# Order of the last share, home of the second residual weights, and engines of the last image in a four-layer kernel

## The chip, the cores and the metric

The kernel runs on one core of one Trainium2 chip. The metric is the device time of one execution in microseconds (us); the text compares medians of several runs, and reads the details from one profiled execution.

## The reference, cut to what matters

Two images of 128 channels and 64 x 64 pixels go through four layers:

```python
x = L0(x)   # group norm, 4-head attention over 4096 pixels, projection, residual
x = L1(x)   # deformable convolutions, below
x = L2(x)   # three residual steps, below
x = L3(x)   # layer norm, selective scan in four directions, projection, residual

# end of layer 1
out = silu(affine(conv2d(concatenate([o0, ox, oy], axis=1), fuse_w, 0), fuse_g, fuse_b))
n = out.shape[2] * out.shape[3] - 1
d = (out - out.mean(axis=(2, 3), keepdims=True)) ** 2
e = d / (4.0 * (d.sum(axis=(2, 3), keepdims=True) / n + 0.0001)) + 0.5
out = out * sigmoid(e)
return out + x

# layer 2
for _ in range(3):
    t = relu(conv(x, w1) + b1)
    x = x + (1.0 / 3.0) * (conv(t, w2) + b2)
return relu(x)
```

The 1 x 1 convolution of layer 1 over three concatenated inputs is a sum of three shares. The two 3 x 3 convolutions of layer 2 have their own weights w1 and w2, used in each of three steps.

## The kernel before

**Engines and order.** PE multiplies matrices, DVE, ACT and POOL do elementwise work, SP issues nearly all DMAs. Each engine works through its own queue in order. Most stages stand under `tc.manual_schedule()`: the order of the Python calls is the order on each engine. A tile that is made where an older pool's tiles lay waits until that pool's instructions are done.

**The attention** (`attend`, layer 0) walks through units (batch b, head h, block of queries qb, block of keys kb), three blocks of keys at a time: `scores` on PE, exponential on ACT, `weigh` on PE, and at the end of each qb `normalise` on DVE and POOL. The queries and keys of the next head are fetched in pieces at qb 1 to 4 of the head before it. At qb 5 to 7 of batch 0, head 3, the kernel loads the three rows of taps of w1 (`residual_taps`, on SP, into the two-buffer pool of the pieces) and combines them on DVE (`residual_weights`, which calls `quad_weights` with ten instructions) into `g.u1`. The 3 x 3 convolutions of layer 2 are computed four columns at a time from six combinations of columns and six combinations of weights, hence the 6 in `u1`.

**The last share** (end of `snakes`, layer 1). For each of eight jobs, one batch and two row blocks j and j + 1, `last_share` gives four parts: `silu` (ACT line 1094, then PE line 1100 into PSUM), `add` (DVE line 1105, two instructions, into the image `xa`), `fused` (ACT line 1109, Silu in place on the image), and `stats` (DVE line 1113, two instructions; after a batch's last job `gate_stats`, lines 1165 to 1169). `by_column` shows the image as four planes of every fourth column, so that the row blocks of one batch lie between one another in memory, and the two batches lie apart. The jobs are put one step apart:

```python
jobs = [last_share(b, j, c) for b in range(NB) for j in range(0, NBLK, 2)]
for n in range(len(jobs) + 3):
    for k in range(4):
        if 0 <= n - k < len(jobs):
            jobs[n - k][k]()
```

**Layer 2** (`layer2`) first makes the gate of layer 1: squares and sigmoids on ACT (lines 1286, 1287), product and sum on DVE (1291, 1292), with the layer's input `gt` loaded on SP (line 1285). Then `products` (PE line 1311) multiplies six combined images `v[j][b]` with six combined weights, `outputs` (lines 1320 to 1347) turns the six results into four columns on ACT and DVE, and `combine` (DVE, lines 1259 to 1270) with `differences` (POOL) prepares the next convolution. `later` runs a combine one turn late. Convolution j is 0 with weights `g.u1` and 1 with weights `u2`; the taps of w2 are loaded as `raw` into a free part of `v[1][1]`, and `quad_weights` (lines 1178 to 1187) makes `u2` from them between `products(0, 1, 1)` and the combines behind it. In the last step both halves k of an image stand in `mid[0]` and `mid[1]`, and after k = 1 two Relus on ACT (line 1347) write them back into the image `xa` in its usual order of pixels, which means with a stride of four elements. Relus of the two batches are made alike.

**Layer 3** (`layer3`) begins with loads of weights on SP, small set-up on DVE (`onesm`, line 1452) and a layer norm that starts on PE (line 1519); then it runs 64 blocks whose loads are `dd`, `b` and `c`.

Of the kernel before, what the change touches and what calls it, by code (L numbers as in the profile page):

```python
# [10 lines left out]
F32 = mybir.dt.float32  # L11
# [9 lines left out]
P = 128  # L21
# [51 lines left out]
def vec(g, name):  # L73
    i = VI[name]
    return g.vecs[:, i : i + 1]
# [6 lines left out]
def layer0(g, I):  # L82
# [6 lines left out]
    with ExitStack() as ctx:  # L89
# [213 lines left out]
        with cond.Else():  # L303
            nc.gpsimd.memset(v3[1][:, :, :, 3 * CH :], 1.0)
            with tc.tile_pool(name="l0vs", bufs=2) as vs, tc.tile_pool(name="l0vp", bufs=2, space=PSUM) as vp:
                for k in range(NBLK):
                    late_values(g, v3, vp.tile([P, BLK], F32, name="pv"), vs, wv, 1, k)
                for y in range(3):
                    residual_weights(g, y, residual_taps(g, I, vs, y))
            nc.vector.memset(g.last[0:96], 0.0)  # L310
            nc.vector.memset(g.last[96:128], 1.0)
            nc.vector.memset(g.heads, 0.0)
            attend_any(g, I, v3, qd, kd, q4)
# [14 lines left out]
    return t  # L328


def residual_taps(g, I, pool, y):

    t = pool.tile([P, PIECE], F32, name="piece")[:, : 3 * P].rearrange("p (x o) -> p x o", o=P)
    g.nc.sync.dma_start(t, I["w1T"][:, 3 * y : 3 * y + 3, :])
    return t


def residual_weights(g, y, t):

    quad_weights(g, g.u1[:, y : y + 1], t.unsqueeze(1), 1.0)  # L340


def normalise(g, acc, rec, parts, dst):
# [60 lines left out]
def attend(g, I, v3, wv, qd, kd, q4, qk, stg):  # L404


    nc, tc = g.nc, g.tc
    NS = L // P
    GR = 3
    LAG = 2  # L410
    with ExitStack() as ctx:
        ap = ctx.enter_context(tc.tile_pool(name="l0ap", bufs=1))
        sm = ctx.enter_context(tc.tile_pool(name="l0asm", bufs=2))
        ep = ctx.enter_context(tc.tile_pool(name="l0ep", bufs=5))
        pss = ctx.enter_context(tc.tile_pool(name="l0pss", bufs=2, space=PSUM))
        psa = ctx.enter_context(tc.tile_pool(name="l0psa", bufs=2, space=PSUM))

        att = {}

        def scores(group):  # L420
            ps = pss.tile([P, GR, BLK], F32, name="ps")
            for i, (b, h, qb, kb) in enumerate(group):
                t = qk[h % 2]
                nc.tensor.matmul(  # L424
                    ps[:, i, :], t[:, 1, kb * P : (kb + 1) * P], t[:, 0, qb * BLK : (qb + 1) * BLK],
                    start=True, stop=True,
                )
            e = ep.tile([P, GR, BLK], F16, name="e16")
            n = len(group)
            nc.scalar.activation(e[:, :n, :], ps[:, :n, :], AF.Exp, scale=1.0 / UP**2)  # L430
            return e

        acc = None

        def weigh(group, e):
            nonlocal acc
            for i, (b, h, qb, kb) in enumerate(group):
                if kb == 0:
                    acc = psa.tile([P, BLK], F32, name="acc")
                nc.tensor.matmul(acc, v3[b][:, kb, h, :], e[:, i, :], start=(kb == 0), stop=(kb == NS - 1))  # L440
                if kb == NS - 1:
                    finish(b, h, qb, acc)

        def finish(b, h, qb, acc):

            if qb == h == 0:
                att[b] = ap.tile([P, L], F32, name="att")
            final = (b, qb) == (NB - 1, NBLK - 1)
            if final and h == NH - 1:
                nc.scalar.copy(g.last, acc)  # L450
                return
            to = g.heads if final else att[b][:, qb * BLK : (qb + 1) * BLK]
            rec = sm.tile([P, BLK], F32, name="rec")
            parts = sm.tile([CH, 3, BLK], F32, name="parts")
            normalise(g, acc, rec, [parts[:, j, :] for j in range(3)], to[h * CH : (h + 1) * CH])
            if h == NH - 1:
                done.append((b, qb))

        def pieces(n, qb):

            if n == 0 and qb == 0:
                return [(0, 0, 1), (0, 0, 2)]
            if n == 0 and qb == 5:
                return [(0, 0, 3)]
            if n + 1 < NB * NH and 1 <= qb <= 4:
                return [(n + 1, 1, qb - 1), (n + 1, 0, qb - 1)]
            return []

        units = [
            (b, h, qb, kb) for b in range(NB) for h in range(NH) for qb in range(NBLK) for kb in range(NS)  # L470
        ]
        held, done, coming = [], [], []
        taps = None
        with tc.manual_schedule():
            nc.gpsimd.memset(v3[1][:, :, :, 3 * CH :], 1.0)
            for c in range(1, 4):
                split_less(g, qk[0], 1, c, q4[1][:, c * PIECE : (c + 1) * PIECE], nc.vector)
            for u in range(0, len(units), GR):
                group = units[u : u + GR]
                b, h, qb, kb = group[0]  # L480
                held.append((group, scores(group)))
                if done and 24 <= kb < 24 + GR:
                    b0, q0 = done.pop(0)
                    project(g, b0, q0, psa.tile([P, BLK], F32, name="acc"), att[b0][:, q0 * BLK : (q0 + 1) * BLK])
                if len(held) > LAG:
                    weigh(*held.pop(0))
                if b == 0 and 1 <= h <= 2 and qb in (0, 5, 6, 7) and 24 <= kb < 24 + GR:
                    k = 4 * (h - 1) + (0, 5, 6, 7).index(qb)
                    late_values(g, v3, psa.tile([P, BLK], F32, name="acc"), sm, wv, 1, k)
                if 4 <= kb < 4 + GR:  # L490
                    coming = [(n, j, c, fetch(g, stg, (qd, kd)[j], n, c)) for n, j, c in pieces(b * NH + h, qb)]
                    if (b, h) == (0, NH - 1) and qb >= 5:
                        taps = qb - 5, residual_taps(g, I, stg, qb - 5)
                elif 26 <= kb < 26 + GR:
                    for n, j, c, t in coming:
                        split(g, qk[n % 2], j, c, t)
                    coming = []
                    if taps:
                        residual_weights(g, *taps)
                        taps = None  # L500
            for x in held:
                weigh(*x)
            assert not done
# [435 lines left out]
def snakes(g, ctx, hz, ahead, fw):  # L939
# [179 lines left out]
    with tc.manual_schedule():  # L1119
# [30 lines left out]
        c, steps = affine(1, st)  # L1150
        for f in steps:
            f()
        jobs = [last_share(b, j, c) for b in range(NB) for j in range(0, NBLK, 2)]
        for n in range(len(jobs) + 3):
            for k in range(4):
                if 0 <= n - k < len(jobs):
# [33 lines left out]
def layer2(g, I):  # L1190
# [14 lines left out]
    with ExitStack() as ctx:  # L1205
# [8 lines left out]

        mid = [a.tile([P, 4, RP, NS], F32, name=f"mid{i}") for i in range(2)]

        raw = v[1][1].rearrange("p x r i -> p (x r i)")[:, 4 * HW * NS : 4 * HW * NS + 9 * P]
        nc.sync.dma_start(raw, I["w2T"].rearrange("p t o -> p (t o)"))
        u2 = a.tile([P, 3, NX, P], F32, name="u2")
        weights = (g.u1, u2)  # L1220
        first = [
# [8 lines left out]
        def inner(t):  # L1230
            return t[:, :, :, 0:NQ]
# [73 lines left out]
        def products(j, b, k):  # L1305
# [8 lines left out]
                    )  # L1314
            return m

        def outputs(step, j, b, k, m):
            s, p = (wk.tile([P, BLK], F32, name=f"m{i}", bufs=2) for i in range(2))
            d, q = (wk.tile([P, BLK], F32, name=f"t{i}") for i in (3, 4))
            nc.scalar.activation(s, m[1], AF.Identity, bias=vec(g, "b1") if j == 0 else b23)  # L1320
            nc.scalar.copy(p, m[3])
            nc.vector.tensor_sub(d, s, m[2])
            nc.vector.tensor_add(s, s, m[2])
            nc.vector.tensor_sub(q, p, m[4])
            nc.vector.tensor_add(p, p, m[4])
            t = mid[k % 2]
            y = [t[:, c, :, 0:NQ] for c in range(4)]
            stt = nc.vector.scalar_tensor_tensor
            stt(y[1], rows_of(q), 2.0, rows_of(d), ALU.mult, ALU.add)
# [11 lines left out]
                where = (v[0][b], k * RP, image[b], k * RP, RP)  # L1341
            else:
                nc.vector.tensor_add(inner(t), inner(t), xv)
                if k == NK - 1:
                    for n in range(NK):
                        out = interior(g, b, n * RP, RP).rearrange("p r (i c) -> p c r i", c=4)
                        nc.scalar.activation(out, inner(mid[n]), AF.Relu)
                where = None
            return where

# [9 lines left out]
        with tc.manual_schedule():  # L1360
# [12 lines left out]
            t1 = gate_differences(0, 1)  # L1373
            gate_weight(0, 2)
            gate_weight(0, 3)
            gate_combine(0, 0, t0)
            gate_combine(0, 1, t1, (0, 2))
            m00 = products(0, 0, 0)
# [26 lines left out]
            later(w01)  # L1405
            w10 = outputs(0, 0, 1, 0, m10)
            m11 = products(0, 1, 1)
            quad_weights(g, u2, raw.rearrange("p (y x o) -> p y x o", y=3, x=3), 1.0 / 3.0)
            for e in (0, HP - 1):
                nc.gpsimd.memset(v[1][1][:, :, e, :], 0.0)  # L1410
            later(w10)
# [621 lines left out]
def body(ctx, tc, I, out, layers=(0, 1, 2, 3), dump=None):  # L2033
# [20 lines left out]
    with tc.tile_pool(name="l2w", bufs=1) as pool:  # L2054
# [4 lines left out]
        g.last = g.lead[:, 576:1088]  # L2059
        g.heads = g.lead[:, 1088:1600]  # L2060
        g.wpt = g.lead[:, 1600:]
        layer0(g, I)
        dr = ctx.enter_context(tc.tile_pool(name="dr", bufs=1, space=bass.MemoryType.DRAM))
        g.xs = [dr.tile([P, L], F32, name=f"xs{b}") for b in range(NB)]
# [120 lines left out]
```

## Time and profile before

| | |
|---|---|
| time, median of 3 runs (lowest to highest) | 5403.01 us (5402.75 to 5405.15) |
| profiled execution: time, span of the core | 5404.17 us, 5402.3 us |
| granted TensorE clock, mean over the span | 0.904 |
| busy, share of the span | PE 85%, DVE 84%, ACT 77%, POOL 67% |
| last share, from 1685 to 1723 us | 38 us |
| layer 2, from 1723 to 2135 us | 412 us |
| layer 3, from 2135 us to the end | 3267 us |

Times in the text are microseconds from the start of the span. "L1109" is line 1109 of the kernel before. A row of the timeline gives start, busy time, engine, line, operation, written and read tiles by name, shapes and number of instructions; the brackets at its end give the idle time before it and what ended that. Most float32 products are two PE instructions each, so counts of matmuls are twice those in the code. Consecutive instructions overlap a little, so that the time from one start to the next is shorter than the busy time of one.

### The profile page before, as it was taken

How to read it: one execution, taken by the hardware profiler on the slowest of the kernel's cores; microseconds unless marked ns; L12 is line 12 of the kernel's file. 1: busy time of each engine (PE TensorE's matmuls, PEld its weight loads, DVE VectorE, ACT ScalarE, POOL GpSimd, SP SyncE). 2: the span in 40 equal slices, each digit the busy share in tenths (PEclk: the TensorE clock that was granted, in tenths of full speed). 3: DMA queues.
4: the chain of work that ended last, by engine and by line, in shares of the span. 5: the costliest groups of instructions: out<-in, count | busy, mean ns of one | idle time of the engine just before them, and what ended most of it. 6: DMA issues, size and time to landing. Idle time of an engine off the chain costs nothing.

```text
span 5402.3 us, 54711 instructions
## 1 busy us (share of the span) xinstructions
PE 4587.6 (85%) x17062; PEld 1704.7 (32%) x17062; DVE 4516.5 (84%) x4281; ACT 4143.2 (77%) x6591; POOL 3593.7 (67%) x1204
## 2 busy tenths in 40 slices
PE   7999999999997998787777878877877778777776
PEld 3444444444453443222222222222222222222221
DVE  7666655572255996899999999999999999999999
ACT  4999999600365113889899899889899899899897
POOL 5232222200000110899999999999999999999999
PEclk9999999999998999888888888888888888888887
DMA  4111110300473000655655565565565565565554
GB/s 170 47 40 35 41 32 24 52 21 16 91 143 70 7 0 7 153 132 129 149 137 132 140 146 130 136 150 135 139 149 133 131 150 133 134 142 142 136 139 110
DMA packets 331018, 554.09 MB, mean 103 GB/s; under 512 B 53456, under 2 KB 112736, under 8 KB 330720
## 3 DMA queue, kind: packets, MB, share of 16 engines
q1 hardware_dynamic: 329568, 549.86, 42.8%
q8 instruction: 135, 2.21, 0.2%
q14 instruction: 163, 1.34, 0.1%
q10 hardware_dynamic: 1152, 0.68, 0.0%
HBM read 461.20 MB, written 89.13 MB: 102 GB/s over the span
## 4 chain that ended last, share of the span: by engine, by line
PE 34%; DVE 32%; DMA 11%; ACT 11%; issue 5%; POOL 4%; SPq 1%; DVEq 0%; ACTq 0%; POOLq 0%
DVE db L1756 20%; DVE db L1715 9%; PE ps L424 9%; PE acc L440 8%; PE m L1311 6%; PE m L715 5%; DMA dd<-dx 5%; DMA c<-bx 4%; ACT da L1739 4%; POOL db L1767 3%; PE acd L1027 2%; PE m L675 1%; DVE gt L1784 1%; ACT db L1748 1%; DMA dx<-dd 1%
## 5 line engine op out<-in xcount | busy, mean ns | idle before, releaser
L1767 POOL TENSOR_TENSOR db<-db,c 128x2048 f32<-128x2048 f32 x511 | 2307.1, 4536 | 21.4 <-ACT hl L1761 19.5
L1756 DVE TENSOR_TENSOR_SCAN db<-da,db 128x512 f32<-128x512 f32 x1725 | 1982.2, 1201 | 20.7 <-ACT db L1748 14.5
L1739 ACT ACTIVATE da<-dd,am 128x512 f32<-128x512 f32 x2048 | 1406.0, 687 | 189.6 <-DVE db L1756 181.1
L1775 PE MATMUL py<-db,fold 128*32 128x512 f32 x4096 | 648.4, 719 | 402.2 <-POOL db L1767 400.3
L430 ACT ACTIVATE e<-ps 128x1536 f16<-128x1536 f32 (+1 forms) x683 | 919.7, 1630 | 23.4 <-PE ps L424 23.4
L1715 DVE TENSOR_TENSOR db<-pbc,dd 128x2048 f32<-128x2048 f32 (+1 forms) x384 | 804.5, 2095 | 31.3 <-DMA dd<-dx 31.3
L1724 POOL TENSOR_TENSOR db<-b,dd 128x2048 f32<-128x2048 f32 (+1 forms) x192 | 727.4, 3789 | 12.6 <-DMA b<-bx 12.6
L1748 ACT ACTIVATE db<-da,db,hl 128x1 f32<-128x1 f32 x1469 | 516.6, 352 | 121.7 <-DVE db L1715 65.1
L424 PE MATMUL ps<-q 128*128 128x512 f16 x2048 | 553.2, 378 | 3.2 <-issue 2.1
L440 PE MATMUL acc<-e,v 128*128 128x512 f16 x2048 | 552.9, 379 | 0.1
L352 POOL TENSOR_TENSOR parts<-parts 32x512 f32<-32x512 f32 x63 | 79.1, 1256 | 654.9 <-DVE parts L351 654.9
L1362 POOL MEMSET v<- 128x256 f32 x2 | 1.1, 548 | 623.2 <-DVE b L1210 623.2
L1311 PE MATMUL m<-v,u 128*128 128x512 f32 x864 | 377.2, 599 | 34.5 <-DVE v L1261 34.2
L1756 DVE TENSOR_TENSOR_SCAN db<-da,hl,db 128x512 f32<-128x512 f32 x323 | 401.2, 1257 | 5.3 <-POOL db L1724 4.6
L346 DVE RECIPROCAL rec<-acc 32x512 f32<-32x512 f32 x63 | 211.6, 3358 | 201.2 <-PE acc L440 200.9
L1662 PE MATMUL pm<-dd,ident 128*128 128x512 f32 x512 | 334.8, 788 | 3.0 <-ACT dd L1655 2.7
L1775 PEld LDWEIGHTS py<-db,fold 128*32 128x32 f32 x4096 | 90.5, 116 | 766.5 <-POOL db L1767 636.6
L424 PEld LDWEIGHTS <-q 128*128 128x128 f16 x2048 | 197.2, 97 | 273.2 <-issue 92.1
L440 PEld LDWEIGHTS <-v 128*128 128x128 bf16 x2048 | 198.9, 97 | 248.4 <-issue 9.3
L1648 PE MATMUL pm<-xd,wdt 8*128 8x512 f32 x256 | 128.4, 866 | 148.9 <-ACT xd L1627 124.7
L1311 PEld LDWEIGHTS m<-v,u 128*128 128x128 f32 x864 | 165.8, 192 | 246.0 <-issue 229.8
L1597 PE MATMUL pm<-xt,wcs 128*128 128x512 f32 x512 | 233.6, 598 | 1.2 <-ACT xa L1808 1.1
(364 smaller groups left out, 6492.0 us busy)
## 6 DMA issues: line engine op xcount, KB each, us to landing
dd<-dx SPq DMA_DIRECT2D x1024, 256.0 KB, 6.5
dx<-dd SPq DMA_DIRECT2D x128, 512.0 KB, 5.1
c<-bx SPq DMA_DIRECT2D x1024, 64.0 KB, 2.1
b<-bx SPq DMA_DIRECT2D x512, 64.0 KB, 4.2
early<-pos SPq DMA_DIRECT2D x104, 256.0 KB, 10.0
piece<-qd SPq DMA_DIRECT2D x128, 128.0 KB, 2.7
piece<-kd SPq DMA_DIRECT2D x112, 128.0 KB, 2.7
hats<-pos SPq DMA_DIRECT2D x32, 256.0 KB, 10.8
```

What stands on the lines that cost most here:

```text
L424: nc.tensor.matmul(ps[:, i, :], t[:, 1, kb * P : (kb + 1) * P], t[:, 0, qb * BLK : (qb + 1) * BLK], start=True, stop=True,)
L430: nc.scalar.activation(e[:, :n, :], ps[:, :n, :], AF.Exp, scale=1.0 / UP**2)
L440: nc.tensor.matmul(acc, v3[b][:, kb, h, :], e[:, i, :], start=(kb == 0), stop=(kb == NS - 1))
L1311: nc.tensor.matmul(m[x], weights[j][:, dy, x, :], v[j][b][:, x, r0 : r0 + RP, :].rearrange("p r i -> p (r i)"), start=(dy == 0), stop=(dy ...
L1662: nc.tensor.matmul(ps, g.ident, S[i]["dd", hf][:, x, :], start=(x == 0), stop=(x == 1))
L1715: nc.vector.tensor_tensor(db_tile(k)[:, :, :n], G[k].pop("pb")[:, :n].unsqueeze(1).to_broadcast([P, 4, n]), S[i]["d4", hf][:, 1, :, :n], A ...
L1724: nc.gpsimd.tensor_tensor(db_tile(k)[:, :, n:], S[i]["b", ng][:, n:].unsqueeze(1).to_broadcast([P, 4, BLK - n]), S[i]["d4", hf][:, 1, :, n ...
L1739: nc.scalar.activation(da, S[i]["d4", hf][:, 0, q, :], AF.Exp, scale=am[:, hf, q, ng : ng + 1])
L1748: nc.scalar.activation(b0, a0, AF.Identity, bias=b0, scale=hl[:, hf, ng, q, :])
L1756: nc.vector.tensor_tensor_scan(d1, d0, d1, 0.0 if zero else hl[:, hf, ng, q, :], ALU.mult, ALU.add)
L1767: eng.tensor_mul(v, v, S[i]["c", ng].unsqueeze(1).to_broadcast([P, 4, BLK]))
L1775: nc.tensor.matmul(S[i]["y", hf][32 * q : 32 * q + 32, :], fold, G[k]["db"][:, q, :], start=False, stop=(ng == NNG - 1),)
```

## The change

Three edits are made at once.

1. The eight jobs of the last share alternate between the two batches.
2. The taps of w2 are combined inside the attention, at qb 5 to 7 of batch 0, head 3, into `g.u1`, and each of the three rows is then stored to a new DRAM tile `g.u2d`. The taps of w1 are combined at qb 5 to 7 of batch 1, head 0, into `g.u1`, where they stay. Layer 2 loads `u2` from DRAM; its load of `raw` and its call of `quad_weights` go. The DRAM pool of `u2d` is opened ahead of all other DRAM pools. The other branch of the attention, which isn't taken here, is changed likewise.
3. In the last step, batch 0's two Relus are issued after the Identity and the copy of batch 1's first half. Batch 1's halves are built in `late`, two tiles in the memory of `v[0][0]`, and written to the image by DVE (k = 1, a maximum with 0) and by ACT (k = 0, a Relu).

```diff
-def residual_weights(g, y, t):
-    quad_weights(g, g.u1[:, y : y + 1], t.unsqueeze(1), 1.0)
+def residual_weights(g, j, y, t):
+    quad_weights(g, g.u1[:, y : y + 1], t.unsqueeze(1), (1.0, 1.0 / 3.0)[j])
+    if j:
+        g.nc.sync.dma_start(g.u2d[:, y], g.u1[:, y])
...
-                    if (b, h) == (0, NH - 1) and qb >= 5:
-                        taps = qb - 5, residual_taps(g, I, stg, qb - 5)
+                    if (b, h) in ((0, NH - 1), (1, 0)) and qb >= 5:
+                        taps = 1 - b, qb - 5, residual_taps(g, I, stg, 1 - b, qb - 5)
...
-        jobs = [last_share(b, j, c) for b in range(NB) for j in range(0, NBLK, 2)]
+        jobs = [last_share(b, j, c) for j in range(0, NBLK, 2) for b in range(NB)]
...
-        raw = v[1][1].rearrange("p x r i -> p (x r i)")[:, 4 * HW * NS : 4 * HW * NS + 9 * P]
-        nc.sync.dma_start(raw, I["w2T"].rearrange("p t o -> p (t o)"))
         u2 = a.tile([P, 3, NX, P], F32, name="u2")
...
+        late = [
+            v[0][0].rearrange("p x r i -> p (x r i)")[:, n * 4 * RP * NS : (n + 1) * 4 * RP * NS].rearrange(
+                "p (c r i) -> p c r i", r=RP, i=NS
+            )
+            for n in range(NK)
+        ]
+        def image_rows(b, n):
+            return interior(g, b, n * RP, RP).rearrange("p r (i c) -> p c r i", c=4)
...
+            final = step == 2 and j == 1
             nc.scalar.activation(s, m[1], AF.Identity, bias=vec(g, "b1") if j == 0 else b23)
             nc.scalar.copy(p, m[3])
+            if final and b and k == 0:
+                for n in range(NK):
+                    nc.scalar.activation(image_rows(0, n), inner(mid[n]), AF.Relu)
...
-            t = mid[k % 2]
+            t = late[k] if final and b else mid[k % 2]
...
                 nc.vector.tensor_add(inner(t), inner(t), xv)
-                if k == NK - 1:
-                    for n in range(NK):
-                        out = interior(g, b, n * RP, RP).rearrange("p r (i c) -> p c r i", c=4)
-                        nc.scalar.activation(out, inner(mid[n]), AF.Relu)
+                if b and k == NK - 1:
+                    nc.vector.tensor_scalar(image_rows(b, 1), inner(late[1]), 0.0, None, ALU.max)
+                    nc.scalar.activation(image_rows(b, 0), inner(late[0]), AF.Relu)
...
             gate_weight(0, 3)
+            nc.sync.dma_start(u2, g.u2d)
...
-            quad_weights(g, u2, raw.rearrange("p (y x o) -> p y x o", y=3, x=3), 1.0 / 3.0)
...
+        wd = ctx.enter_context(tc.tile_pool(name="wd", bufs=1, space=bass.MemoryType.DRAM))
+        g.u2d = wd.tile([P, 3, 6, P], F32, name="u2d")
         layer0(g, I)
```

More of the change, by code (lines that the diff above doesn't have):

```diff
@@ L307, in layer0 @@
                     late_values(g, v3, vp.tile([P, BLK], F32, name="pv"), vs, wv, 1, k)
-                for y in range(3):
-                    residual_weights(g, y, residual_taps(g, I, vs, y))
+                for j in (1, 0):
+                    for y in range(3):
+                        residual_weights(g, j, y, residual_taps(g, I, vs, j, y))
             nc.vector.memset(g.last[0:96], 0.0)
@@ L328, in fetch, with residual_taps @@
     return t
-def residual_taps(g, I, pool, y):
+def residual_taps(g, I, pool, j, y):
     t = pool.tile([P, PIECE], F32, name="piece")[:, : 3 * P].rearrange("p (x o) -> p x o", o=P)
-    g.nc.sync.dma_start(t, I["w1T"][:, 3 * y : 3 * y + 3, :])
+    g.nc.sync.dma_start(t, I[("w1T", "w2T")[j]][:, 3 * y : 3 * y + 3, :])
     return t
-def residual_weights(g, y, t):
-    quad_weights(g, g.u1[:, y : y + 1], t.unsqueeze(1), 1.0)
+def residual_weights(g, j, y, t):
+    quad_weights(g, g.u1[:, y : y + 1], t.unsqueeze(1), (1.0, 1.0 / 3.0)[j])
+    if j:
+        g.nc.sync.dma_start(g.u2d[:, y], g.u1[:, y])
 def normalise(g, acc, rec, parts, dst):
```

## The prediction

> **What bounds the kernel now.** I read the page first (busy shares, slices, chain), then busy time by stage, and then, inside the three stages that the change touches, the timeline, the waits of single lines and the chain of waits in order of time. The table of stages (start:end, length, then busy time of PE, PEld, DVE, ACT, POOL with instruction counts, granted clock, DMA share, GB/s):
>
> ```profile
> 1685.00:1723.00 38.00, 17.93 (x32) 6.52 (x32) 22.37 (x45) 22.57 (x20) 0.57 (x3) 0.83 0.09 28
> 1723.00:1815.00 92.00, 68.26 (x149) 29.50 (x150) 88.17 (x150) 35.17 (x29) 21.69 (x31) 0.88 0.14 41
> 1815.00:2124.00 309.00, 308.96 (x716) 136.26 (x715) 275.48 (x407) 48.73 (x51) 48.04 (x36) 0.99 0.00 0
> 2124.00:2135.00 11.00, 0.06 (x1) 0.09 (x1) 3.36 (x4) 7.93 (x3) 0.00 (x0) 0.62 0.00 0
> ```
>
> The fused sum (1685 to 1723) keeps no engine busy: it is a chain of waits. The start of layer 2 (to 1815) is DVE's, 88 of 92 us; then PE is full for 309 us; then 11 us belong to a short tail in which PE does nothing. The attention before has PE full and DVE partly idle; layer 3 behind (2200 to 3000) has DVE busy 793 of 800 us, so it follows its own start rigidly.
>
> What makes the fused sum wait is in the answer for line 1109, the in-place Silu on ACT (idle of its engine by releaser, then who waited for it):
>
> ```profile
>   DVE xa L1105: 11.5, 6
> ...
>   DVE st L1113: 7.0, 6
>   DVE xa L1105: 1.3, 1
> ```
>
> and in the timeline:
>
> ```profile
> 1701.39 1.24 ACT L1109 ACTIVATE xa<-xa,vecs 128x1024 f32<-128x1024 f32 x1 [1.47 <-DVE xa L1105]
> 1703.87 1.27 DVE L1105 TENSOR_TENSOR xa<-xa,pf 128x512 f32<-128x512 f32 x2
> 1704.05 1.24 ACT L1109 ACTIVATE xa<-xa,vecs 128x1024 f32<-128x1024 f32 x1 [0.28 <-DVE st L1113]
> 1722.33 1.20 ACT L1286 ACTIVATE v<-xa,stat 128x1088 f32<-128x1088 f32 x1 [2.15 <-DVE stat L1169]
> ```
>
> At 1701.39 the Silu of job 2 starts at the end of job 3's add (1700.03 to 1701.30), though its own add ended at 1697.45: jobs of one batch write interleaved columns of one image, and one job's Silu is held for the next job's add, and statistics for the next job's Silu. At 1704.05 the Silu of job 3 (batch 0) runs beside the add of job 4 (batch 1, from 1703.87): across batches there is no such wait.
>
> The two other places, first u2's ten combining instructions on DVE with PE waiting for them, then the tail:
>
> ```profile
> 1807.51 0.55 DVE L1178 TENSOR_TENSOR u<-v 128x384 f32<-128x384 f32 x1
> 1809.99 1.95 PE L1311 MATMUL m<-v,u 128*128 128x512 f32 x4 [0.35 <-DVE u L1181]
> 1812.33 0.41 DVE L1187 TENSOR_SCALAR u<-v 128x384 f32<-128x384 f32 x1
> 1814.72 35.87 PE L1311 MATMUL m<-v,u 128*128 128x512 f32 x79 [2.77 <-DVE v L1261]
> 2124.73 2.29 DVE L1343 TENSOR_TENSOR mid<-mid,xa 128x2048 f32<-128x2048 f32 x1
> 2127.05 7.48 ACT L1347 ACTIVATE xa<-mid 128x2048 f32<-128x2048 f32 x2 [10.19 <-DVE mid L1343]
> 2134.63 0.17 DVE L1452 MEMSET onesm<- 128x128 f32 x1 [7.61 <-ACT xa L1347]
> 2134.94 5.45 PE L1519 MATMUL da<-xa,onesm 128*128 128x512 f32 x6 [10.97 <-DVE onesm L1452]
> ```
>
> Layer 3's first instructions on DVE, SP and PE all start behind the last Relu.
>
> **A. Batches alternate in the last share.** No work is added. Per job DVE needs an add pair (1.19 us to the next instruction, 1706.52 to 1707.71) and a statistics pair (1.31, 1707.71 to 1709.02), 2.5 us; ACT needs Silu (1.15) and in-place Silu (1.25), 2.4 us. So DVE can set the pace if nothing holds it. With neighbours in different batches, the in-place Silu of job n waits only for its own add and the statistics of job n-2; the add of job n for the in-place Silu of job n-2; each was issued a whole step earlier. The first three Silus and their matmuls stay (PE at its slow start, matmuls of job 2 end at 1695.9), so add 2 ends at 1696.6. From there DVE has eight statistics pairs (10.5), five add pairs (5.95) and the two gate statistics (0.74 and 0.82): 18.0 us, to 1714.6, against 1722.23 now. **Gain 7.6 us**; 8.3 if all DVE waits behind line 1109 go (7.0 + 1.3), 6.2 if one of its 1.37 us waits stays. Layer 2's gate (line 1286) waits for the statistics of batch 1 in either order, since its tile takes the memory that they use. Its table load (1.28 us, after the last in-place Silu) still ends earlier than they do. The first image loads (gt, issued at 1710.22 when the last Silu of line 1094 ended) move up with that Silu by some 5 us, and land 4.2 us later, before their use at 1726.22 less 7.6.
>
> **B. Second weights.** Layer 2 loses ten DVE instructions (1807.51 to 1812.66: 5.15 us) and a 576 KB load that nobody was seen waiting for. The combine behind them then starts at 1807.5 in today's times; its line 1261, which releases PE, ends 2.05 us later at 1809.55, before PE ends its last matmuls at 1809.64. PE so loses both waits, 0.35 + 2.77, and the four matmuls between run at the full 0.43 us each (308.96 us over 716; 1.72 in place of 1.95): **gain 3.35 us**. The other 1.8 us go nowhere: PE is the bound behind 1814.72. Lower end 2.5, should line 1262 or 1267 come in late; above 3.35 there is nothing.
>
> Its price is in the attention: three more combinings of ten instructions in (batch 1, head 0), 2.5 us each (541.53 to 543.99 for batch 0, head 3), three 192 KB loads, three 384 KB stores. The cover is DVE's idle time. In 650 to 692 us, where they will lie, DVE works 17.7 of 42 us and PE all 42. They are queued ahead of a normalise; in batch 0, head 3, with the same order, DVE then still waits for PE:
>
> ```profile
> 543.77 0.22 DVE L1187 TENSOR_SCALAR u<-piece 128x128 f32<-128x128 f32 x1
> 544.02 0.33 SPq L334 DMA_DIRECT2D piece<-in_w1T  x1
> 545.39 3.36 DVE L346 RECIPROCAL rec<-acc 32x512 f32<-32x512 f32 x1 [1.40 <-PE acc L440]
> ```
>
> On SP each store waits for the combining on DVE, and behind it stand the next taps and then the first pieces that batch 1, head 0 loads ahead. Today these are issued at 544.02, 558.13 and 573.43, the moment a combining frees their buffer, so the store costs them its issue, some 0.4 us; the taps are used 11 us later, the pieces a block of 14 us or more later. I take **0**; without the cover it would be 3 x 2.5 = 7.5 us, and no gain is possible, as nothing leaves PE or ACT there. The load of u2 (1152 KB) stands on SP behind the two gt loads (issue 1727.5 to 1730.8 today) and ahead of a gt load that waits for DVE until 1739.58. By twice the 4.2 us of a 544 KB load it lands in about 9 us; its first reader is PE 75 us later. Cost 0.
>
> **C. Last image.** Batch 0's two Relus move behind the Identity and copy of batch 1's first half: ACT then runs them from about 2098 to 2105.5, free until 2111.13. DVE's wait for ACT there (8.15 us before line 1322) goes, worth nothing since PE is unbroken to the end. At the end, one Relu of 2048 (3.84 us; pitch 3.64) and one maximum on DVE start together at 2127.0 in place of two Relus. DVE's form isn't in the trace: 2048 dense elements of tensor_scalar take 1.23 us (line 936); an add that writes at a stride (line 1083) takes 1.056 against 0.68 dense, 1.7 times per element; so 2.1 us from the one, 3.9 from line 1343's 2.29 times 1.7, 4.6 at double. Against ACT's 3.84 only the last matters. **Gain 3.6 us**, 2.9 with the slowest maximum; 1.4 if ACT had to wait for a 2.2 us maximum. They write different rows of one image, and PE's line 188 started at 17.48 behind the first of eight row-block writes (line 181, 16.61 + 0.80), so rows are told apart and I don't expect that.
>
> The Trainium skill speaks against the DVE half: "SBUF — State Buffer", section "Door 1: The DMA port swizzle", says in its note on cachelines that each access that crosses to a new 16-byte line pays a penalty, and this store puts every f32 into a new line. The trace agrees for ACT: 3.84 us here against 1.92 for the dense Relu of the same size (line 1337). By that rule at its worst, twice the slow form, the sum would be 0.7 us smaller.
>
> **Sum:** 7.6 + 3.35 + 3.6 = 14.55 us. The profiled execution took 5404.17 (span 5402.3 and 1.9 around it) and becomes 5389.6; from the median of the runs, 5403.01, that is **5388.5**. A measurement of this kernel can tell about 0.2%, 10.8 us, from no change; the forecast is 0.27%.
>
> **Rivals.**
> - *Part of it is lost on the way* (0.16, within 0.2%). Either the waits of line 1109 go on across batches: A falls to about 0, the sum to 7, time 5396; against it is 1704.05 above. Or the combinings in the attention stop PE for their 7.5 us: also 5396; against it is the 1.40 us of slack. Or layer 3's first block takes up some 5 us because its loads or clock don't move with its start: 5393.5; against it, its loads are issued at 2134.6 behind the same Relu.
> - *Slower* (0.05). The new DRAM tile of 1.18 MB is allocated ahead of all others, so every later DRAM tile moves, those of layer 3 too (the trace can't show what an address costs). Loads of dd and c carry 9% of the chain, some 480 us over 64 blocks, 7.6 us a block. If they became 10% slower and DVE waited for it, 0.76 us a block, 49 us: 5437. It decides from 0.40 us a block on, where (14.55 + 10.8) us are eaten. Against it: after the first block DVE hardly waits for a load (31.3 us once, at the start).
> - *The maximum on DVE and the Relu run one after the other*: 5390.7, still faster; it is in the range.
> - *The change doesn't do what it says*: if u2 came late, B would turn into a wait; 75 us of slack speak against it. Its chance is in the first rival.
>
> **How the numbers follow.** The forecast with the third rival has 0.79. Smallest sum of the bounds: 6.2 + 2.5 + 1.4 = 10.1, 5392.9; largest: 8.3 + 3.35 + 3.64 = 15.3, 5387.7. Runs spread by 2.4 us, and layer 3's start may shift by a few either way: 5385 to 5394.5, which takes in the mild end of the first rival and leaves out its 5396 and the slow case. Faster by over 0.2% (under 5392.2) 0.79, within 0.16, slower 0.05.
>
> **What would show it.** Right: line 1109 idle behind line 1105 and line 1113 behind it nearly gone, L1286 some 7.6 us earlier; no DVE u line in layer 2 and PE unbroken from products of batch 1 into the second convolution; one Relu beside one DVE maximum at the end and layer 3 some 14.5 us earlier in all. PE still full around 650 to 692. Wrong: a gap of PE in the attention behind the new combinings, L1292 or L1311 waiting for a DMA, a maximum of over 4 us, or a DVE share of layer 3 that falls below today's 99%.

## The result and the profile after

Faster, by 0.35%: the median of seven runs of the kernel after is 5386.65 us (5384.31 to 5390.22), that of seven runs of the kernel before beside them 5405.15 us (5402.75 to 5410.15). The ratio is 0.9965, with a 95% interval of 0.9953 to 0.9977. The forecast was 5388.5 us, in a range of 5385.0 to 5394.5. The profiled execution after took 5387.11 us with a span of 5385.3 us, 17.0 us less than the span of before; the mean granted clock is 0.905 against 0.904.

Line numbers move: what was L1105, L1109, L1113 and L1286 is now L1108, L1112, L1116 and L1287; L1261 and L1311 are now L1262 and L1312; the last Relu stands at L1361 and the new maximum at L1360. The same stages as before, in the same columns (start:end, length, busy time of PE, PEld, DVE, ACT, POOL, granted clock, DMA share, GB/s):

```profile
1685.00:1715.00 30.00, 18.64 (x36) 7.65 (x36) 21.56 (x46) 22.33 (x20) 0.00 (x0) 0.79 0.13 37
1715.00:1803.00 88.00, 67.78 (x147) 29.54 (x148) 83.61 (x145) 34.14 (x27) 21.89 (x32) 0.86 0.17 49
1803.00:2113.00 310.00, 308.19 (x719) 136.02 (x717) 278.19 (x410) 50.72 (x54) 48.02 (x36) 1.00 0.00 0
2113.00:2120.00 7.00, 1.44 (x2) 0.84 (x3) 4.98 (x8) 5.16 (x2) 0.00 (x0) 0.68 0.08 27
```

DVE and ACT do about the same work in the fused sum in a shorter stage; the start of layer 2 is shorter by about the time that DVE works less there; in the last stage DVE and ACT now work side by side, where ACT worked 7.93 of 11 us, mostly alone.

Cut at the starts of instructions that both kernels have, the two profiled executions differ like this (first exponential L430, last matmul of `weigh` L440, first Silu L1094 of the last share, first square L1286, last add L1334 of the last products, `onesm` L1452, in lines of before; differences are taken before rounding):

| stage, us | before | after | difference |
|---|---|---|---|
| start to first exponential | 103.8 | 105.7 | +1.9 |
| attention | 933.0 | 933.3 | +0.3 |
| layer 1 up to the last share | 649.7 | 650.0 | +0.3 |
| last share, to the first square | 35.8 | 27.4 | -8.4 |
| layer 2, to the last add | 401.7 | 394.8 | -6.8 |
| tail, to `onesm` | 10.6 | 7.0 | -3.6 |
| layer 3 | 3267.7 | 3267.1 | -0.6 |

The three stages of the change give 18.8 us; 1.9 us go at the start, where nothing was forecast.

**Last share.** What the in-place Silu waited for, after (L1112; idle time of ACT by releaser, us and times):

```profile
  DVE st L1116: 2.9, 3
  DVE xa L1108: 2.6, 2
```

In the kernel before, these were 11.5 us behind L1105 alone, and DVE waited 7.0 + 1.3 us for this line. Now DVE doesn't stand among those that wait for it. The timeline shows the new pace:

```profile
1704.97 1.27 DVE L1108 TENSOR_TENSOR xa<-xa,pf 128x512 f32<-128x512 f32 x2
1705.14 1.24 ACT L1112 ACTIVATE xa<-xa,vecs 128x1024 f32<-128x1024 f32 x1
1706.15 1.28 DVE L1116 BATCH_NORM_STATS2 st<-xa 128x6 f32<-128x512 f32 x2
1707.35 1.27 DVE L1108 TENSOR_TENSOR xa<-xa,pf 128x512 f32<-128x512 f32 x2
...
1716.38 1.20 ACT L1287 ACTIVATE v<-xa,stat 128x1088 f32<-128x1088 f32 x1 [1.55 <-DVE stat L1172]
```

Silu of one batch runs beside the add of the other, none of these four rows shows a wait, and DVE takes 2.38 us a job from one add to the next (1704.97 to 1707.35).

**Layer 2 and tail.** PE in the products, and the end of the last image:

```profile
1767.62 17.27 PE L1312 MATMUL m<-v,u 128*128 128x512 f32 x36 [2.72 <-DVE v L1262]
1786.49 63.77 PE L1312 MATMUL m<-v,u 128*128 128x512 f32 x148 [1.60 <-DVE v L1262]
...
2111.95 2.29 DVE L1358 TENSOR_TENSOR v<-v,xa 128x2048 f32<-128x2048 f32 x1
2114.28 3.88 ACT L1361 ACTIVATE xa<-v 128x2048 f32<-128x2048 f32 x1 [10.19 <-DVE v L1358]
2114.28 2.03 DVE L1360 TENSOR_SCALAR xa<-v 128x2048 f32<-128x2048 f32 x1
2118.24 0.17 DVE L1466 MEMSET onesm<- 128x128 f32 x1 [1.94 <-ACT xa L1361]
```

From the products of batch 1's second half on (1786.49) PE has no gap: 148 instructions in 63.77 us, 0.431 us each. At the end both engines start at 2114.28, and `onesm` waits for ACT's 3.88 us alone.

**Attention.** At qb 5 of batch 1, head 0, the timeline shows the start of the new combining, an instruction of POOL beside it, the last instruction of the combining and DVE's next one:

```profile
656.04 0.75 DVE L1181 TENSOR_TENSOR u<-piece 128x128 f32<-128x128 f32 x1
656.71 1.25 POOL L356 TENSOR_TENSOR att<-parts 32x512 f32<-32x512 f32 x1
656.82 1.30 DVE L1182 TENSOR_TENSOR u<-u,piece 128x128 f32<-128x128 f32 x1
...
659.75 0.22 DVE L1190 TENSOR_SCALAR u<-piece 128x128 f32<-128x128 f32 x1
664.17 3.36 DVE L349 RECIPROCAL rec<-acc 32x512 f32<-32x512 f32 x1 [4.20 <-PE acc L443]
```

DVE then still waits 4.20 us for PE, and PE stays full (42.00 of 42.00 us from 650 to 692): the cover holds. The work under it was larger than forecast. A combining takes 3.9 us here (656.04 to 659.97) and not 2.5, with 0.75 and 1.30 us for its first two instructions beside POOL's part of `normalise`, against 0.28 and 0.29 at 543.66, where POOL does nothing. DVE works 29.71 us of the 42, in place of 17.73.

### The profile page after: what moved, and what is told of

It is laid out like the page before. It is cut to its first block, busy times and chain, and to the rows that moved or that the text cites. A ratio compares the mean times of both kernels' runs of the same rounds, so it can differ in the third digit from the quotient of the medians.

```text
span 5385.3 us, 54741 instructions
## 1 busy us (share of the span) xinstructions
PE 4593.3 (85%) x17062; PEld 1702.9 (32%) x17062; DVE 4526.1 (84%) x4302; ACT 4141.7 (77%) x6590; POOL 3592.8 (67%) x1204
## 4 chain that ended last, share of the span: by engine, by line
PE 34%; DVE 32%; DMA 12%; ACT 10%; issue 5%; POOL 4%; SPq 1%; DVEq 0%; POOLq 0%; ACTq 0%
DVE db L1770 20%; DVE db L1729 9%; PE ps L427 9%; PE acc L443 8%; PE m L1312 6%; PE m L718 5%; DMA dd<-dx 5%; DMA c<-bx 5%; ACT da L1753 4%; POOL db L1781 2%; PE acd L1030 2%; PE m L678 1%; DVE gt L1798 1%; DMA dx<-dd 1%; POOL db L1738 1%
## 5 line engine op out<-in xcount | busy, mean ns | idle before, releaser
L1312 PE MATMUL m<-v,u 128*128 128x512 f32 x864 | 376.0, 598 | 25.7 <-DVE v L1262 25.7
L1635 PE MATMUL pm<-u,wxp 128*72 128x512 f32 x256 | 148.0, 708 | 109.7 <-ACT u L1616 109.7
L1312 PEld LDWEIGHTS m<-v,u 128*128 128x128 f32 x864 | 165.6, 192 | 236.1 <-issue 223.5
```

Of the source, the lines that this page charges most:

```text
L1312: nc.tensor.matmul(m[x], weights[j][:, dy, x, :], v[j][b][:, x, r0 : r0 + RP, :].rearrange("p r i -> p (r i)"), start=(dy == 0), stop=(dy ...
```

## The experiments

**1 to 4: each part alone.** The first three kernels are the kernel before with one part of the change; the fourth is the kernel before itself.

```diff
 e1: -jobs = [... for b in range(NB) for j in range(0, NBLK, 2)]
     +jobs = [... for j in range(0, NBLK, 2) for b in range(NB)]
 e2: the second part alone (taps, store to u2d, load of u2, no quad_weights in layer 2)
 e3: the third part alone (final, late, image_rows, maximum and Relu)
```

> Only the order of the eight jobs is changed. Theory (the waits of one batch's jobs for one another go, and nothing else in the order matters): from the first Silu of the last share (line 1094) to the first square of layer 2 (line 1286) 27.4 us in place of 35.8, the stages behind it as before within 2 us, in all 8 us less (0.15%). Rival (the gain needs the other edits, or is given back in layer 2 because gt loads or the gate come late): the stage shrinks, but layer 2 takes some 3 us or more longer.

> Only the weights are moved to the attention and to DRAM. Theory (PE loses its wait and, with the gap, also a stretch at half clock behind it): from the start of the products of batch 1, second half, to the last add of columns on DVE (line 1334) 5 to 6.8 us less than the 331.6 us of before, the attention (first exponential to the last weigh) as long as before within 0.5 us. Rival 1 (the gain is the wait alone): 3.35 us less. Rival 2 (the combinings in the attention are not hidden): the attention 2 to 7.5 us longer.

> Only the last image is made by two engines. Theory: from the last add of columns (line 1334) to layer 3's first memset (line 1452) 7.0 us in place of 10.6, the rest as before. Rival (layer 3 takes the gain back, since its loads come before anything can use them): the distance shrinks, but from that memset to the end the kernel takes some 3 us longer than the 3267.7 us of before.

> The kernel before, unchanged, to see what another profile of it gives. If the places where PE's clock drops in the start of layer 2 are set by the kernel, the gaps and the slow stretches lie as in the first profile (slow products of batch 1, second half, 17.2 us, fast first half, 15.7); if they are a matter of phase, the slow stretches move while the gaps stay, and the distance from the start of layer 2 to its last add of columns differs by up to 1.7 us. The part up to the first exponential of the attention may differ by 2 us or so in either case.

Medians against the kernel before beside them (5405.73 us, 27 runs): order 5395.54 (ratio 0.9981, 0.9971 to 0.9990), weights 5401.55 (0.9989, 0.9980 to 0.9998), tail 5402.59 (0.9991, 0.9982 to 1.0000), 11 runs each. The parts add up: 0.19 + 0.11 + 0.09 = 0.39%, against 0.35% (0.23 to 0.47) for all three. By stages of the profiles, in us:

| | start | last share | layer 2 | tail |
|---|---|---|---|---|
| e4, before again | 104.0 | 35.6 | 401.7 | 10.6 |
| e1, order | 104.2 | 27.6 | 401.5 | 10.6 |
| e2, weights | 104.8 | 35.7 | 394.9 | 10.6 |
| e3, tail | 104.5 | 35.8 | 401.7 | 7.0 |

Of the last three columns each part moves its own and no other, by 8.0 to 8.2, 6.8 and 3.6 us; the start is taken up under 11 and 12. So B is worth 6.8 us here and not 3.35, with or without the others. The timeline of PE in the kernel before and in e1, where layer 2 is as before, shows the first half of the reason:

```profile
1792.44 17.20 PE L1311 MATMUL m<-v,u 128*128 128x512 f32 x36 [3.19 <-DVE v L1261]
...
1784.86 15.69 PE L1311 MATMUL m<-v,u 128*128 128x512 f32 x36 [1.52 <-DVE v L1261]
1802.42 1.95 PE L1311 MATMUL m<-v,u 128*128 128x512 f32 x4 [1.88 <-DVE u L1181]
1807.15 43.44 PE L1311 MATMUL m<-v,u 128*128 128x512 f32 x97 [2.77 <-DVE v L1261]
```

In e1 (from 1784.86) the products of batch 1's second half take 15.69 us and PE waits 1.88 us for u2. In the profile of before (1792.44) they took 17.20 us and the wait was 0.35. Their sums, 17.57 and 17.55, agree: what PE saves in those matmuls it waits for DVE, which sets when u2 is ready. A slow stretch of PE had hidden 1.5 us of the wait that the forecast read as 0.35. The second profile of the kernel before (e4) goes the way of e1, with 15.69 us and a wait of 1.87, and its layer 2 is as long as in the first.

**5: another order of the same jobs.** The kernel after, with two jobs of one batch, then two of the other. It asks whether A is what it was taken for, the waits between neighbours of one batch: 4 of 7 neighbours are now of one batch, against 6 in the kernel before and none in the kernel after.

```diff
-jobs = [last_share(b, j, c) for j in range(0, NBLK, 2) for b in range(NB)]
+jobs = [last_share(b, j + i, c) for j in (0, 4) for b in range(NB) for i in (0, 2)]
```

> The changed kernel, but the jobs of the last share go in pairs of one batch (0, 0, 1, 1, 0, 0, 1, 1), with three changes of batch in place of seven (the kernel before has one). Theory (a job waits for the next job of its own batch and for none of the other): in place of 27.4 us from the first Silu (line 1094) to the first square of layer 2 (line 1286 of before) some 32.5 us, so a part of the waits behind the in-place Silu is back, DVE's between 4 and 6 us in all. Rival (the order helps by having batch 1's work at hand from the start, however it is mixed): 28 us or less. Rival (only strict alternation helps): 35 us or more.

One run, 5391.83 us; its last share takes 32.0 us, 4.6 us more than 27.4, where the kernel before has 8.4 more. 4.6 of 8.4 is 55%, 4 of 6 is 67%: the loss follows the number of such neighbours about. Over all profiles the stage takes 35.1 to 35.8 us in six with the old order and 26.4 to 27.6 us in seven with the new one.

**6 to 8: a gap of PE, by dose.** In the kernel after, which has u2 from DRAM, 4, 10 and 20 instructions of the size of `quad_weights` are put back on DVE where the combining stood; their results go to `gt`, which is free by then, and are not used. Three accounts of B's extra gain stood against each other: the waits alone; that u2 is ready early, whatever DVE does; or the waits and a lower clock of PE behind them.

```diff
             w10 = outputs(0, 0, 1, 0, m10)
             m11 = products(0, 1, 1)
+            spare(n)          # n = 4, 10, 20: as quad_weights, from u2 to gt
```

> The changed kernel with four instructions of the shape of the removed combining put back on DVE at its old place (some 2.25 us), into memory that nobody reads, so that PE waits for the combine behind them but not for weights. From the first square of layer 2 to the last add of columns the changed kernel takes 394.9 us. Theory (a wait of PE costs itself, and where it falls into PE's clock monitor, also a stretch at half clock): a gap of PE of about 2.1 us and 397.0 us, or 398.7 where the clock drops. Rival (the wait alone): 397.0 us and no drop.

> As before, with all ten instructions (5.15 us). Theory: a gap of PE of about 5 us, a slow stretch behind it that costs some 1.7 us, 401.6 us from the first square to the last add of columns, so all that layer 2 gained by the weights is lost again although the weights come from DRAM. Rival 1 (the wait alone): 399.9 us. Rival 2 (the gain came from the weights being there early): 396 us or less.

> As before, with twenty instructions (10.3 us). Theory: a gap of about 10.2 us and the same 1.7 us of slow stretch, since it lasts as long however long the gap: 406.8 us from the first square to the last add of columns. Rival 1 (the slow stretch grows with the gap): 408 us or more. Rival 2 (the wait alone): 405.1 us.

The times (one run each) are 5390.10, 5393.50 and 5397.11 us, and layer 2 takes 397.1, 402.8 and 407.3 us against 394.8. PE's first matmul behind the gap in the timeline, and the granted clock of the 3.5 us from there (the number after POOL's), for 4 instructions:

```profile
1806.16 44.04 PE L1312 MATMUL m<-v,u 128*128 128x512 f32 x102 [1.99 <-DVE v L1262]
```

```profile
1806.20:1809.70 3.50, 3.50 (x8) 1.59 (x9) 3.46 (x6) 0.00 (x0) 0.00 (x0) 1.00 0.00 0
```

for 10:

```profile
1807.02 43.41 PE L1312 MATMUL m<-v,u 128*128 128x512 f32 x94 [4.90 <-DVE v L1262]
```

```profile
1807.00:1810.50 3.50, 3.48 (x4) 1.51 (x5) 3.47 (x6) 0.00 (x0) 0.00 (x0) 0.50 0.00 0
1810.50:1814.00 3.50, 3.50 (x7) 1.58 (x6) 3.43 (x7) 0.00 (x0) 2.65 (x2) 0.69 0.00 0
```

and for 20:

```profile
1811.70 38.48 PE L1312 MATMUL m<-v,u 128*128 128x512 f32 x84 [10.03 <-DVE v L1262]
```

```profile
1811.70:1815.20 3.50, 3.50 (x4) 1.51 (x5) 3.46 (x6) 0.00 (x0) 0.00 (x0) 0.50 0.00 0
1815.20:1818.70 3.50, 3.50 (x9) 1.49 (x8) 3.43 (x7) 0.00 (x0) 2.65 (x2) 0.87 0.00 0
```

Behind 1.99 us the clock stays at 1.00 and layer 2 loses 2.3 us, little more than the gap. Behind 4.90 us it loses 8.0, behind 10.03 us 12.5: 3.1 and 2.5 us more than the gap. The clock rows give most of this: 3.5 x (0.50 + 0.31) = 2.8 us, and 3.5 x (0.50 + 0.13) = 2.2 us, more than the 1.7 us expected. So the waits alone are refuted for the longer gaps, and the price of the slow stretch doesn't grow with the gap. With ten instructions the whole of B is gone, though u2 comes from DRAM: early weights are worth nothing, DVE's time is what counts.

The same rows exist in the profile of before, first behind the gap of 3.19 us ahead of the products of batch 1's second half, then behind the 2.77 us that the change removes:

```profile
1792.40:1796.00 3.60, 3.56 (x5) 1.71 (x6) 3.53 (x9) 1.80 (x3) 0.00 (x0) 0.57 0.00 0
1814.70:1818.20 3.50, 3.48 (x6) 1.61 (x7) 3.46 (x6) 0.00 (x0) 0.00 (x0) 0.68 0.00 0
1818.20:1822.00 3.80, 3.80 (x8) 1.56 (x8) 3.73 (x7) 0.00 (x0) 2.65 (x2) 0.84 0.00 0
```

The second stretch costs 3.5 x 0.32 + 3.8 x 0.16 = 1.7 us, and nothing behind it waits, so it is lost in full. The first costs 3.6 x 0.43 = 1.5 us, which the wait for u2 hid. The Trainium skill, "TensorE: Matmul & The Clock Gate", section "Part 1: The HAM clock gate (the 'warmup' mystery)", says that the array falls to half its clock after an idle window of about 3.4 us and returns to full after a busy one, and that the window runs freely, so that the phase decides. The trace agrees on the half clock (0.50 here), on its length (it is over after two such rows) and on the phase: in before, the gap of 3.57 us at 1773.56 left the clock at 1.00. It differs on the idle time: gaps of 2.72 (after, 1767.62, clock 0.53 in the row from there) and 2.77 us were enough.

**9 and 10: a balanced tail, and the kernel after beside it.** ACT was last by 1.94 us at the end, so DVE takes 10 rows of ACT's 32.

```diff
-nc.scalar.activation(image_rows(b, 0), inner(late[0]), AF.Relu)
+part = 22
+rest = interior(g, b, part, RP - part).rearrange("p r (i c) -> p c r i", c=4)
+head = interior(g, b, 0, part).rearrange("p r (i c) -> p c r i", c=4)
+nc.vector.tensor_scalar(rest, inner(late[0])[:, :, part:, :], 0.0, None, ALU.max)
+nc.scalar.activation(head, inner(late[0])[:, :, :part, :], AF.Relu)
```

> The changed kernel with the last image shared out by the engines' measured rates: DVE's maximum took 2.03 us for 32 rows beside ACT's 3.88, so DVE takes 42 rows (two instructions) and ACT 22. Theory: both end some 2.7 us after the last add, the distance from the last add of columns to layer 3's first memset is 5.9 us in place of 7.0, 1.1 us less in all, too little for the times alone to show. Rival (both engines write to the same lines of memory at a stride and slow one another the more evenly they are loaded): 6.5 us or more.

> The changed kernel, unchanged, beside e9 on the same chip and for another profile of the start of layer 2. If the forecast's stages are right: 27.4 us, 394.9 us (or up to 1.7 us more, if the slow stretch of PE falls on the products of batch 1, second half), 7.0 us and 3267 us for last share, layer 2, tail and layer 3.

The tail takes 5.9 us in the profile against 7.0 beside it: the Relu is 2.74 us long, and DVE's second maximum ends (2117.92) just ahead of it.

```profile
2115.32 2.74 ACT L1365 ACTIVATE xa<-v 128x1408 f32<-128x1408 f32 x1 [10.19 <-DVE v L1358]
2117.20 0.72 DVE L1364 TENSOR_SCALAR xa<-v 128x640 f32<-128x640 f32 x1
```

Its median is 5383.82 us (5 runs, 5380.85 to 5387.22), ratio 0.9962 (0.9949 to 0.9976); the kernel after beside it 5386.31 us (6 runs, 5384.11 to 5388.00), 0.9968 (0.9956 to 0.9980), against 5403.21 us before (10 runs). It is the best version, by 1.1 us of the profile; the times alone don't tell the two apart.

The second profile of the kernel after also shows how the clock's phase moves a run. Its timeline of PE:

```profile
1765.60 15.69 PE L1312 MATMUL m<-v,u 128*128 128x512 f32 x36 [3.27 <-DVE v L1262]
1784.48 55.15 PE L1312 MATMUL m<-v,u 128*128 128x512 f32 x124 [3.20 <-DVE v L1262]
```

PE's products of batch 1's first half went at full speed (36 in 15.69 us, against 17.27 in the first profile), the gap behind them grew to 3.20 us, the slow stretch fell behind that one, where nothing hides it, and layer 2 took 396.6 us against 394.8. So part of B hangs on this phase. With u2 from DRAM and no added instructions, layer 2 takes 394.8 to 394.9 us in four profiles and 396.6 in this one; with `quad_weights` in layer 2 it takes 401.5 to 401.7 in all six. B is worth 6.8 us in four profiles and 5.1 in the fifth.

**11 and 12: the start.** The first exponential comes at 103.8 to 104.5 us in the four profiles so far without the second part of the change, and at 104.8 to 106.2 us in the eight with it. Experiment 11 gives the kernel before the DRAM tile alone, experiment 12 the additional instructions alone (the first weights are combined twice).

```diff
 e11: +wd = ...; g.u2d = wd.tile([P, 3, 6, P], F32, name="u2d")
      +nc.sync.dma_start(g.u2d[:, 0, 0], u2[:, 0, 0])       # in layer 2
 e12: -if (b, h) == (0, NH - 1) and qb >= 5:
      +if (b, h) in ((0, NH - 1), (1, 0)) and qb >= 5:
```

> The kernel before with the new 1.18 MB DRAM tile allocated and one small store into it in layer 2, nothing else of the change. Asked: where the 1.5 us at the start come from (start to the first exponential 103.8 to 104.5 us in four profiles without the weights' edit, 104.8 to 106.2 in eight with it; cast of the flag, line 298, at 101.1 to 101.8 against 102.0 to 103.5). If the tile's place in memory moves what the first loads read, the cast of line 298 comes at 102 to 103.5 and the first exponential at 105 to 106, as in the kernels with the edit. If it is the longer program (30 more DVE instructions, six more transfers), both stay at 101 to 102 and 104. The median is 5405 to 5407 either way.

> The kernel before, which combines the first residual weights a second time in (batch 1, head 0), with the same numbers: 30 more DVE instructions and three more 192 KB loads in the attention, no DRAM tile, no stores, layer 2 and its raw load as before. Asked: the start again, now that the tile alone left it at 104.3 us. If more instructions in the program cost the first loads their pace, the first exponential comes at 105 to 106 us and the cast of line 298 at 102 to 103.5. If it takes the stores and the reload of the second weights, or nothing but chance of the run, 104 and 101 to 102. The attention stays at 933.0 to 933.6 us, since DVE's idle time covers the combining; if the combining stopped PE there it would be up to 7.5 us longer. Median 5405 to 5408.

The first exponential comes at 104.3 us with the tile and at 105.0 us with the instructions, one profile each. The DMA traffic of the first 20 us parts the two groups more widely; with the tile and with the instructions:

```profile
DMA packets 2948, 6.21 MB, mean 311 GB/s; under 512 B 662, under 2 KB 1046, under 8 KB 2948
```

```profile
DMA packets 2569, 5.44 MB, mean 272 GB/s; under 512 B 639, under 2 KB 1023, under 8 KB 2569
```

The five profiles without a second set of combinings in the attention have 311 to 319 GB/s there, the nine with it 272 to 289 (316 before, 289 after). The chip isn't the cause: the two chips that ran kernels of both kinds have 313 to 319 against 282 on the one, 311 against 281 and 288 on the other. So the tile's place doesn't bring it about, and the stores and the load of u2 aren't needed for it. It goes with the longer program of the attention, some 600 us before the first of the added instructions runs; by which way that reaches the first loads no run shows. The first exponential comes 1.4 us later (means of 104.2 and 105.6 us), though the two groups lie only 0.3 us apart at their edges. The attention of e12 takes 933.0 us: three more combinings are free there, as forecast. Its time is 5406.23 us, and that of e11 5408.23, one run each beside 5407.14 and 5405.67 of the kernel before, which says no more than that neither is far from it; e11's layer 1 up to the last share took 654.5 us against 647 to 653 in the others, a stage that no edit touches.

## Why the prediction was right, and where it was wrong

**Bound and sign: right.** Each part moved the stage that was read as its own, and layer 3 behind (3266.8 to 3268.4 us in every profile) and the attention ahead (933.0 to 933.7) gave nothing back.

**A: right in mechanism, 0.4 to 0.8 us too small.** Forecast 7.6 us, measured 8.0 to 8.4 in the profiles of the change and of its first part. The waits behind L1109 went in full, which was the upper end (8.3). The mis-sized term is the statistics pair, taken at 1.31 us; back to back it takes 1.20 (1706.15 to 1707.35), and there are eight, 0.9 us in all.

**B: right in mechanism and place, half the size.** The step that failed is "above 3.35 there is nothing", with "The other 1.8 us go nowhere". The waits (3.12 us) and the slower pace of the four matmuls between them (0.23) were counted. Two terms were not: the slow matmuls behind the removed gap (1.7 by the clock rows of before; 1.8 by 72 instructions in 32.86 us, against 31.0 at 0.431 us each), and the wait that the slow products of batch 1's second half had hidden (1.5). 3.35 + 1.8 + 1.5 = 6.65, against 6.8 measured. The last term counts only where the products of batch 1's second half run at full speed; in the second profile of the kernel after they don't, and 3.35 + 1.8 = 5.15 meets the 5.1 measured. The hint stood in the profile of before: 36 instructions in 17.20 us there, and a granted clock of 0.88 in that stage. The prediction compared the pace of four matmuls with that of an unbroken stretch, and not that of the matmuls on both sides of the gaps.

**C: right.** 3.6 us, as forecast. The maximum took 2.03 us, just under the lowest of the three bounds (2.1, 3.9, 4.6), so with its store into every fourth element it takes 1.65 times the dense 1.23 us. (The factor of 1.7 in the prediction is too large as it stands: 1.056 against 0.68 us is 1.55.) The rule on 16-byte lines that the prediction cites from the Trainium skill ("SBUF — State Buffer", section "Door 1: The DMA port swizzle"), taken at its worst, would have made it slower than ACT and the sum 0.7 us smaller. The trace doesn't bear that out for this DVE instruction, while ACT's Relu stays at 3.88 against 1.92 dense. Maximum and Relu ran side by side, so that rival is refuted.

**The costs: right but for the start.** Cost 0 in the attention and 0 for the load of u2 hold (PE unbroken from 1786.49), the first although a combining there took 3.9 us and not 2.5. That the second part would come with slower loads in the first 20 us was not foreseen: 1.4 us more on the mean, 1.9 in this pair.

**The rivals.** Waits across batches: none. PE stopped by the combinings: no stage shows it. A slower layer 3 through moved DRAM addresses: no sign, neither with the tile alone nor in any kernel with it.

**Luck.** For the two profiled executions the errors are +0.75 (A), +3.49 (B), -1.85 (start) and +0.08 (the other stages without an edit): 14.55 + 2.47 = 17.02 us. The errors of B and of the start partly offset each other, so the total came out closer than its terms. The medians differ by 18.5 us, 4 us more than forecast; the time itself came within 1.9 us, because the forecast starts from 5403.01 us, the median of three runs, and that of the seven runs beside the kernel after is 2.1 us higher.

## What to carry to other kernels

A wait of PE that ends on DVE is priced by DVE's whole time in front of it, not by the gap: slow matmuls ahead of the gap may hide part of the wait, and slow ones behind it are lost on top, so read the granted clock on both sides (here 3.1 us of gaps were worth 6.8, or 5.1 where the slow stretch fell elsewhere). Reordering independent jobs so that neighbours touch parts of a tile that lie apart is free time when two engines write in turn into interleaved parts of it. And compare stages cut at shared instructions rather than whole times: only so does a cost of 1.4 us, hundreds of microseconds ahead of the edit, show up.

## What the runs showed of the hardware

- Gaps of PE of 1.5 to 2.0 us left the clock at 1.00 in this stage; most of those of 2.6 to 3.9 us dropped it, three did not (3.57 us in before, 3.58 in e3, 3.27 in the second profile of after); those of 4.90 and 10.03 us dropped it to 0.50. A slow stretch that nothing hides costs 1.7 to 3.1 us, and no more behind the longest gap.
- A DVE maximum of 2048 float32 that writes every fourth element takes 2.03 us, a Relu on ACT with the same store 3.88 us.
- Two DVE instructions of 128 x 128 float32 that took 0.28 and 0.29 us with POOL idle (543.66 in after) took 0.75 and 1.30 us beside two instructions of POOL (655.37 to 657.96).
- Kernels with instructions added to the attention load more slowly in the first 20 us: 272 to 289 GB/s in nine profiles, against 311 to 319 in five. The cause is open.
